# Layer norm's normalisation from VectorE to ScalarE, and tokens and statistics of the QKV stage in another order, in a transformer block on one core

## The chip, the core and the metric

The kernel runs on one core of a Trainium2 chip. The core has a matmul engine (TensorE: PE in the profile, its weight loads PEld), a vector engine (VectorE: DVE), an engine for activations, which computes func(scale * x + bias) with a scale and a bias per partition (ScalarE: ACT), a general engine (GpSimd: POOL), and a queue that only issues transfers (SyncE: SP). Each engine takes its own instructions in order, waits on semaphores for the others, and reads from a working memory of 128 partitions; matmul results go to a small second memory of banks (PSUM). The metric is the device time of one execution in microseconds (us); the time of a kernel is the median of its runs. A profile comes from one execution of its own.

## The reference

The reference is a transformer block whose two layer norms are modulated by a condition. It runs on x of shape (2, 2048, 512) in float32, with 16 heads of 32 channels and a hidden size of 2048:

```python
mod = silu(condition) @ Wada + bada
sh_a, sc_a, gt_a, sh_m, sc_m, gt_m = split(mod, 6, axis=1)
xm = layernorm(x, g1, be1) * (1 + sc_a) + sh_a
x  = x + gt_a * attention(xm, Wqkv, Wproj, bproj)     # causal
xm = layernorm(x, g2, be2) * (1 + sc_m) + sh_m
x  = x + gt_m * (gelu(xm @ W1 + b1) @ W2 + b2)
```

Each layer norm takes the mean and the variance over the 512 channels of a token, subtracts the mean and multiplies by 1 / sqrt(variance + eps). The gains and shifts g, be, sc and sh are folded by the kernel into one scale and one shift per channel (a1, c1, a2, c2), applied after the tokens have been transposed.

## The kernel before

The two batch rows of 2048 tokens go one after the other through three stages, and then the MLP runs over all of them.

**QKV stage** (class `Qkv`). A row has four groups of 512 tokens, a group four tiles of 128. For a group, `norm` makes the normalised, transposed and modulated tokens xmT in two halves: it normalises two tiles in place (x - mean) * rstd (L244), transposes them on PE into PSUM (L211), and returns a function that applies a1 and c1 on the way back, on DVE (L263) and ACT (L268) by turns. `group` then makes 12 products of a group, numbered n = 0 to 11: eight of queries and keys (`ps_qk`, drained by ACT at L833 and by DVE at L834 into a staging tile `hl` of two parts, of which there are four, and stored by SP at L839), then four of values (`ps_v`, drained by ACT at L855 into `vv`). Behind each product, `between(n)` runs. It is there that the next group is made ready: at n = 0 its tokens are requested (`load_x`, L784), at n = 5 and n = 8 its two halves are normalised and transposed. The statistics of a group (`stats`, L215 and L218: bn_stats and bn_aggr on DVE, and then `inv_std`, L221 and L222: the root on ACT, the reciprocal on DVE) are asked for inside `norm` at n = 5 of the group before, for row 0 from its second group on and for row 1 from its third (those of the first group of row 0 are taken at the start, those of the first two of row 1 in the projection stage). After product 1 SP also loads the new group's keys (L316) and queries (L325) back from memory. From a row's second group on, score matmuls (`s<-kst,qst`) are laid between the matmuls of the products from n = 2 on; DVE takes their row maxima (L456 and L461), and PE has two banks for them. In row 1's QKV stage POOL also prepares the MLP's weights, by transfers of its own queue.

**Attention** (`attention_phase`). PE makes scores, exponentials come from ACT (L596), and DVE still takes the maxima of later units. In the last unit `prepare` and `prefetch` load what comes next, among it four tiles in an old query buffer (`next_s`, shown as `qst`): in row 0 the first four token tiles of row 1, in row 1 the first four tiles of the MLP's input (`x1d`).

**Projection** (`project_phase`). Sixteen output tiles, n = 0 to 15; DVE adds the residual (L1052) and takes the statistics of the second norm, and `inv_std` and a further instruction (L1064) leave rstd2 and shift2 = -mean * rstd. Behind tile n, `between(n)` makes the next stage ready: in row 0 the statistics of row 1's first group at n = 0 to 3 and its two halves at n = 5 and 8, and those of the second group's tokens from n = 12 on; in row 1 the first two groups of the MLP (`ln_t`), in halves at n = 5, 7, 11 and 13.

**MLP.** Two passes over 2048 tokens each. The tokens of the second pass are normalised by ACT, two tiles at a time, as scale * x + bias with rstd2 and shift2 (`normed`, L1281).

The order of the instructions on an engine comes from a planner that may move an instruction to where it expects its inputs to be ready. An instruction wrapped in `act(...)` is held in program order among the others of its engine that are so wrapped; matmuls and transposes on PE all are. The normalisation of L244 is not wrapped before the change, so it stands wherever the planner found room on DVE.

Of the kernel before, what the change touches and what calls it, by code (L numbers as in the profile page):

```python
# [17 lines left out]
P = 128  # L18
# [9 lines left out]
def dit_block_kernel(  # L28
# [36 lines left out]
    nc = tc.nc  # L65
    B, T, D = x.shape
# [3 lines left out]
    NT = T // P  # L70
# [3 lines left out]
    MTT = MT // P  # L74
    NG = T // MT
# [5 lines left out]
    const = ctx.enter_context(tc.tile_pool(name="const", bufs=1))  # L81
# [65 lines left out]
    mv1 = const.tile([P, B * NT, 2], F32, tag="mv1", name="mv1")  # L147
    rstd1 = const.tile([P, B * NT], F32, tag="rstd1", name="rstd1")
    mv2 = const.tile([P, B * NT, 2], F32, tag="mv2", name="mv2")
    rstd2 = const.tile([P, B * NT], F32, tag="rstd2", name="rstd2")  # L150
    shift2 = const.tile([P, B * NT], F32, tag="shift2", name="shift2")

    bgate = bp.tile([P, D], F32, tag="bgate", name="bgate")
# [51 lines left out]
    def act(ins):  # L205

        return tc.keep_in_program_order(ins)
# [9 lines left out]
            act(ins)  # L217
        nc.vector.bn_aggr(mv[:, n, :], st)  # L218

    def inv_std(mv, rstd, lo, hi):  # L220
        nc.scalar.activation(rstd[:, lo:hi], mv[:, lo:hi, 1], AF.Sqrt, bias=eps)  # L221
        nc.vector.reciprocal(rstd[:, lo:hi], rstd[:, lo:hi])  # L222

    def rows_of(psum, r, b, tag):

# [1 line left out]
        mm(ps, pick[:, r, b, :], modr, start=True, stop=True)  # L227
        return ps

    def transposed(pool_, psum, xts, n0, mv, rstd, a, c, b, dst, xns=None):  # L230

        count = len(xts)
        per = 512 // (count * P)
        by_act = xns is not None
        xns = xns or []
        for t, xt in enumerate(xts):
            if by_act:  # L240
                continue
            xn = xt
            n = n0 + t
            nc.vector.tensor_scalar(  # L244
                xn, xt, mv[:, n, 0:1], rstd[:, n : n + 1], ALU.subtract, ALU.mult
            )
            xns.append(xn)
        banks = []
        for cc in range(0, C, per):
            ps = psum.tile([P, per, count * P], F32, tag="mm", name="ps_xt")  # L250
            for ci in range(per):
                for t in range(count):
                    transpose(
                        ps[:, ci, t * P : (t + 1) * P],
                        xns[t][:, (cc + ci) * P : (cc + ci + 1) * P],
                    )
            banks.append(ps)

# [13 lines left out]

        return modulate
# [498 lines left out]
    class Qkv:  # L772
# [20 lines left out]
        def stats(self, g, t, keep=False):  # L793

            n0 = self.row.b * NT + g * MTT
            stats(self.qp, self.xts[g][t], n0 + t, mv1, keep)
            if t == MTT - 1:
                inv_std(mv1, rstd1, n0, n0 + MTT)

        def norm(self, g, j):  # L800

            b = self.row.b
            if j == 0:
                if g > b:
                    for t in range(MTT):
                        self.stats(g, t)
                self.xmT[g] = self.qp.tile([P, C, MT], F32, tag="xmT", name="xmT", bufs=2)
            return transposed(
                self.qp, self.psum, self.xts[g][2 * j : 2 * j + 2],
                b * NT + g * MTT + 2 * j, mv1, rstd1, a1, c1, b,  # L810
                self.xmT[g][:, :, j * 2 * P : (j + 1) * 2 * P],
            )

        def group(self, g, hp, between, among):
# [44 lines left out]
        def run(self, hp, also):  # L859

            row = self.row
            for g in range(NG):

                def between(n):
                    if g + 1 < NG:
                        if n == 0 and g + 1 not in self.xts:
                            self.load_x(g + 1)
                        if n in (5, 8):
                            self.norm(g + 1, n // 8)()
                    elif n == 8:  # L870

                        row.rows(0)
                        act(nc.scalar.activation(first, eps, AF.Exp))
                    also(g, n)
# [127 lines left out]
    def project_phase(row, psum, between):  # L1002
# [4 lines left out]
        b = row.b  # L1007
        with pool(f"proj{b}") as pp:
            n = 0
# [50 lines left out]
                    between(n)  # L1060
                    n += 1
        lo, hi = b * NT, (b + 1) * NT
        inv_std(mv2, rstd2, lo, hi)
        nc.vector.scalar_tensor_tensor(  # L1064
            shift2[:, lo:hi], mv2[:, lo:hi, 0], -1.0, rstd2[:, lo:hi], ALU.mult, ALU.mult
        )


    row = Row(0)
# [184 lines left out]
    with ExitStack() as mlp:  # L1254
# [11 lines left out]
        def ln_t(m, g, j, xts, xns=None):  # L1266

            n0 = (2 * m + g) * MTT + 2 * j
            transposed(
                wp, ps_mm, xts, n0, mv2, rstd2, a2, c2, n0 // NT,  # L1270
                xm[:, :, g, j * half_t : (j + 1) * half_t], xns,
            )()

        def normed(m, n, xts):
# [653 lines left out]
```

## Time and profile before

| | |
|---|---|
| median of 3 runs | 2315.9 us (2313.6 to 2324.05) |
| the profiled execution | 2323.64 us, of which 2321.8 us are the span of the profile |
| granted TensorE clock, mean | 0.996 |
| PE busy | 2262.0 us, 97% |
| PEld busy | 1387.3 us, 60% |
| DVE busy | 1579.0 us, 68% |
| POOL busy | 1289.6 us, 56% |
| ACT busy | 915.0 us, 39% |

In the rows of a timeline the first number is the start in us from the beginning of the span, the second the length in us; then come engine, line, operation, output <- input, the shapes, and the count of merged instructions. In square brackets stands how long the engine was idle just before, and after the arrow the instruction that ended this wait. In a table of windows, each row is a stretch of time: its length, the busy us of PE, PEld, DVE, ACT and POOL (with their numbers of instructions), the granted PE clock (1.00 is full speed), the busy share of the transfer engines, and GB/s. A row that counts a group gives the least, median and greatest length in ns and when the first and the last began. Matmuls overlap at their ends, so the lengths of neighbouring rows may add up to more than the time between their starts. Names without a number stand for all buffers of the name.

### The profile page before, as it was taken

What the parts mean: (1) busy time and instruction counts of PE and PEld (TensorE: products, weight loads), DVE (VectorE), ACT (ScalarE), POOL (GpSimd) and SP (SyncE); (2) the same over time, 40 slices, a digit from 0 to 9 for tenths busy, and PEclk for the clock granted to TensorE, in tenths of its full rate; (3) what the DMA queues carried; (4) which work ended last, traced back from release to release, by engine and by line L of the source; (5) the groups of instructions that cost most, each with busy time, mean ns of one, the idle gap of its engine ahead of it and who ended that gap; (6) DMA issues with size and microseconds to landing.
All of it is one profiled execution on the core that took longest, in us unless ns stands there. A gap on an engine that the chain in (4) does not pass through costs nothing. (4 is left out here: it accounts for less than half of the span.)

```text
span 2321.8 us, 33418 instructions
## 1 busy us (share of the span) xinstructions
PE 2262.0 (97%) x12141; PEld 1387.3 (60%) x12141; DVE 1579.0 (68%) x3117; ACT 915.0 (39%) x1744; POOL 1289.6 (56%) x1036
## 2 busy tenths in 40 slices
PE   8999999999999999999999998999999999999998
PEld 3455455455544444454455554446888888788787
DVE  3366776777756635577677777555896876876787
ACT  2112555555555011155555554622332242152230
POOL 1052987878793664468788885554663602602510
PEclk9999999999999999999999999999999999999999
DMA  7577216151224799970522304265376654654543
GB/s 254 185 243 206 56 27 134 29 119 47 84 107 144 234 301 312 330 192 24 119 47 54 89 24 138 78 218 203 119 266 214 207 178 145 202 184 155 199 143 116
DMA packets 118524, 355.60 MB, mean 153 GB/s; under 512 B 14496, under 2 KB 15052, under 8 KB 103640
## 3 DMA queue, kind: packets, MB, share of 16 engines
q1 hardware_dynamic: 107040, 293.64, 42.0%
q0 software_dynamic: 10944, 59.28, 7.0%
q8 instruction: 96, 1.57, 0.3%
q14 instruction: 68, 0.56, 0.1%
q10 hardware_dynamic: 376, 0.55, 0.1%
HBM read 253.80 MB, written 107.48 MB: 156 GB/s over the span
## 5 line engine op out<-in xcount | busy, mean ns | idle before, releaser
L596 ACT ACTIVATE e<-st 128x512 f32<-128x512 f32 (+1 forms) x1152 | 573.7, 579 | 405.5 <-PE st L203 363.6
L461 DVE TENSOR_REDUCE mx<-s 128x1 f32<-128x512 f32 x612 | 413.4, 687 | 190.3 <-PE s L203 189.1
L626 POOL TENSOR_TENSOR ee<-ee,e 128x1024 f32<-128x1024 f32 x212 | 498.8, 2384 | 12.3 <-ACT e L596 12.3
L203 PE MATMUL s<-kst,qst 128*128 128x512 f32 (+3 forms) x1032 | 473.6, 460 | 20.7 <-DVE mx L461 9.9
L203 PE MATMUL st<-qst,kst 128*128 128x512 f32 (+3 forms) x1280 | 401.9, 379 | 0.0
L203 PE MATMUL ps_a<-sum,room 128*128 128x256 f32 x1504 | 357.3, 382 | 8.8 <-DVE c L1412 6.2
L203 PEld LDWEIGHTS ps_a<-sum,room 128*128 128x128 f32 x1504 | 281.3, 190 | 58.5 <-issue 11.4
L203 PE MATMUL o<-e,vv 128*32 128x512 f32 (+3 forms) x2560 | 301.1, 539 | 0.9 <-POOL e L605 0.9
L456 DVE CUSTOM_DVE_ANT_0 junk<-s,causal 128x128 bf16<-128x128 f32 (+3 forms) x420 | 206.2, 491 | 121.8 <-PE s L203 114.1
L203 PEld LDWEIGHTS s<-kst,qst 128*128 128x128 f32 x1032 | 194.6, 189 | 154.8 <-issue 66.1
L203 PEld LDWEIGHTS st<-qst,kst 128*128 128x128 f32 x1280 | 229.5, 189 | 68.9 <-issue 39.6
L626 POOL TENSOR_TENSOR ee<-e 128x1024 f32<-128x1024 f32 x84 | 198.2, 2381 | 123.2 <-ACT e L596 123.2
L203 PE MATMUL ps_qk<-xmT,wqkv 128*128 128x512 f32 x512 | 239.0, 594 | 1.8 <-DVE xmT L263 1.8
L605 POOL TENSOR_SCALAR_AFFINE_SELECT e<-e 128x256 f32<-128x256 f32 x256 | 103.9, 435 | 112.5 <-ACT e L596 110.3
L203 PEld LDWEIGHTS ps_qk<-xmT,wqkv 128*128 128x128 f32 x512 | 93.9, 190 | 97.2 <-issue 90.9
L203 PEld LDWEIGHTS <-sel 32*128 32x128 bf16 x1152 | 29.8, 91 | 197.0 <-issue 194.9
L1640 POOL TENSOR_TENSOR c<-c,h 128x512 f32<-128x512 f32 x40 | 58.0, 1470 | 160.8 <-ACT c L1638 160.8
L203 PE MATMUL ps_b<-sum,room 128*128 128x256 f32 x608 | 143.6, 379 | 0.0
L203 PEld LDWEIGHTS ps_b<-sum,room 128*128 128x128 f32 x608 | 115.0, 190 | 15.4
L203 PE MATMUL ps_v<-wqkv,xmT 128*128 128x512 f32 x256 | 123.7, 600 | 0.0
L203 PE MATMUL st<-fold,sel 32*128 32x512 bf16 (+1 forms) x1152 | 118.5, 373 | 4.3 <-DVE mhl L482 2.8
L203 PEld LDWEIGHTS o<-e,vv 128*32 128x32 f32 x2560 | 61.3, 108 | 98.9 <-issue 80.8
(179 smaller groups left out, 2949.5 us busy)
## 6 DMA issues: line engine op xcount, KB each, us to landing
qst<-q SPq DMA_DIRECT2D x128, 256.0 KB
room<-w1e SPq DMA_DIRECT2D x28, 1024.0 KB
kst<-k SPq DMA_DIRECT2D x24, 1024.0 KB
room<-w1e SPq DMA_DIRECT2D x28, 768.0 KB
room<-w2e SPq DMA_DIRECT2D x21, 1024.0 KB
q<-hl SPq DMA_DIRECT2D x32, 512.0 KB
k<-hl SPq DMA_DIRECT2D x32, 512.0 KB
room<-w2e SPq DMA_DIRECT2D x21, 768.0 KB
```

The source lines that it names most:

```text
L203: return tc.keep_in_program_order(nc.tensor.matmul(*args, **kw))
L456: nc.vector.tensor_tensor_reduce(junk[:, :w], s[:, :w], causal[:, QB - w :], 1.0, MASKED, ALU.add, ALU.max, m,)
L461: nc.vector.tensor_reduce(m, s[:, :w], axis=AX.X, op=ALU.max)
L596: act(nc.scalar.activation(e[:, h % 2, :w], sts[h][:, :w], AF.Exp))
L605: nc.gpsimd.affine_select(d, d, pattern=[[0, 2], [1, P]], compare_op=ALU.is_ge, fill=0.0, base=0, channel_multiplier=-1,)
L626: act(engine.tensor_tensor(dst, x, y, ALU.add))
L1640: nc.gpsimd.tensor_tensor(c, c, piece_of(base, i, t, pair), ALU.add)
```

## The change

Four things are done. `inv_std` can also make shift = -mean * rstd, and does so for the first norm (shift1, a new small tile) as it was done by hand for the second. `transposed` normalises, where it is given a shift, on ACT as rstd * x + shift instead of on DVE, and either form is now held in program order; all calls give the shift but that of row 0's first group, which stays on DVE. The tokens of group g + 2 are requested at n = 9 of group g instead of at n = 0 of group g + 1. The statistics of a row's third and fourth group are taken one tile per product, at n = 1 to 4 of the group before, and held in program order; those of row 0's second group stay together at n = 5, and are held in program order too.

```diff
-    def inv_std(mv, rstd, lo, hi):
+    def inv_std(mv, rstd, lo, hi, shift=None):
         nc.scalar.activation(rstd[:, lo:hi], mv[:, lo:hi, 1], AF.Sqrt, bias=eps)
         nc.vector.reciprocal(rstd[:, lo:hi], rstd[:, lo:hi])
+        if shift is not None:
+            nc.vector.scalar_tensor_tensor(
+                shift[:, lo:hi], mv[:, lo:hi, 0], -1.0, rstd[:, lo:hi], ALU.mult, ALU.mult
+            )
...
         for t, xt in enumerate(xts):
             if by_act:
                 continue
-            xn = xt
             n = n0 + t
-            nc.vector.tensor_scalar(
-                xn, xt, mv[:, n, 0:1], rstd[:, n : n + 1], ALU.subtract, ALU.mult
-            )
-            xns.append(xn)
+            if shift is None:
+                act(
+                    nc.vector.tensor_scalar(
+                        xt, xt, mv[:, n, 0:1], rstd[:, n : n + 1], ALU.subtract, ALU.mult
+                    )
+                )
+            else:
+                act(
+                    nc.scalar.activation(
+                        xt, xt, AF.Identity,
+                        bias=shift[:, n : n + 1], scale=rstd[:, n : n + 1],
+                    )
+                )
+            xns.append(xt)
...
             if t == MTT - 1:
-                inv_std(mv1, rstd1, n0, n0 + MTT)
+                inv_std(mv1, rstd1, n0, n0 + MTT, shift1)
...
             if j == 0:
-                if g > b:
+                if (b, g) == (0, 1):
                     for t in range(MTT):
-                        self.stats(g, t)
+                        self.stats(g, t, True)
...
                 self.xmT[g][:, :, j * 2 * P : (j + 1) * 2 * P],
+                shift=shift1 if b or g else None,
             )
...
                     if g + 1 < NG:
                         if n == 0 and g + 1 not in self.xts:
                             self.load_x(g + 1)
+                        if 1 <= n <= MTT and g >= 1:
+                            self.stats(g + 1, n - 1, True)
                         if n in (5, 8):
                             self.norm(g + 1, n // 8)()
+                        if n == 9 and g + 2 < NG:
+                            self.load_x(g + 2)
...
-        inv_std(mv2, rstd2, lo, hi)
-        nc.vector.scalar_tensor_tensor(
-            shift2[:, lo:hi], mv2[:, lo:hi, 0], -1.0, rstd2[:, lo:hi], ALU.mult, ALU.mult
-        )
+        inv_std(mv2, rstd2, lo, hi, shift2)
...
             transposed(
                 wp, ps_mm, xts, n0, mv2, rstd2, a2, c2, n0 // NT,
-                xm[:, :, g, j * half_t : (j + 1) * half_t], xns,
+                xm[:, :, g, j * half_t : (j + 1) * half_t], xns, shift2,
             )()
```

More of the change, by code (lines that the diff above doesn't have):

```diff
@@ L150, in dit_block_kernel @@
     rstd2 = const.tile([P, B * NT], F32, tag="rstd2", name="rstd2")
+    shift1 = const.tile([P, B * NT], F32, tag="shift1", name="shift1")
     shift2 = const.tile([P, B * NT], F32, tag="shift2", name="shift2")
@@ L228, in rows_of, with transposed @@
         return ps
-    def transposed(pool_, psum, xts, n0, mv, rstd, a, c, b, dst, xns=None):
+    def transposed(pool_, psum, xts, n0, mv, rstd, a, c, b, dst, xns=None, shift=None):
         count = len(xts)
```

## The prediction

> **What bounds the kernel now.** I read, in this order, the shares of the engines, the busy times stage by stage, then PE's idle gaps in order of time, and last what DVE, ACT and the clock do around each gap.
>
> ```profile
> PE 2262.0 (97%) x12141; PEld 1387.3 (60%) x12141; DVE 1579.0 (68%) x3117; ACT 915.0 (39%) x1744; POOL 1289.6 (56%) x1036
> core 0: us, PE busy (x) PEld busy (x) DVE busy (x) ACT busy (x) POOL busy (x), PEclk, DMA share, GB/s
> 19.00:214.00 195.00, 194.94 (x569) 95.23 (x569) 101.22 (x248) 38.59 (x69) 40.67 (x55) 1.00 0.69 216
> 214.00:739.20 525.20, 516.62 (x3666) 260.77 (x3665) 365.08 (x871) 303.68 (x608) 404.28 (x281) 1.00 0.32 81
> 796.90:996.00 199.10, 191.55 (x534) 94.18 (x532) 98.89 (x238) 35.84 (x65) 104.38 (x132) 0.99 0.93 311
> 996.00:1530.70 534.70, 519.52 (x3666) 261.60 (x3665) 371.22 (x875) 304.00 (x608) 404.43 (x281) 0.99 0.32 81
> ```
>
> PE is busy 97% of the span. The stages are the QKV products of batch row 0, its attention, and the same two of row 1. In row 0's QKV stage PE has no gap at all (194.94 of 195.00): whatever makes PE wait there is paid in full. Row 1 runs the same 3666 attention matmuls in 534.70 us that row 0 runs in 525.20, and its QKV stage has 7.55 us of gaps. Here are these gaps, each behind the DVE or ACT row that caused it:
>
> ```profile
> 847.44 0.69 DVE L215 BATCH_NORM_STATS2 stat<-x 128x6 f32<-128x512 f32 x1 [9.05 <-DMA x<-in_x_dram]
> 852.66 0.44 PE L203 MATMUL s<-kst,qst 128*128 128x384 f32 x1 [2.15 <-DVE mx L456]
> 892.21 0.69 DVE L215 BATCH_NORM_STATS2 stat<-x 128x6 f32<-128x512 f32 x1 [5.18 <-DMA x<-in_x_dram]
> 899.39 0.50 PE L203 MATMUL s<-kst,qst 128*128 128x512 f32 x1 [2.61 <-DVE mx L461]
> 933.91 0.60 ACT L833 ACTIVATE hl<-ps_qk 128x512 fp32r<-128x512 f32 x1 [3.98 <-DMA k<-hl]
> 935.88 0.64 PE L203 MATMUL s<-kst,qst 128*128 128x512 f32 x1 [2.79 <-DVE mx L461]
> 1418.62 2.47 DVE L244 TENSOR_SCALAR qst<-qst,mv,rstd 128x512 f32<-128x512 f32 x1 [3.15 <-DMA qst<-x1d]
> 1421.74 0.26 PE L522 MATMUL ps_m<-ident_h,mhl 128*128 128x128 bf16 x1 [4.37 <-DVE mx L461]
> 1431.50 3.79 DVE L244 TENSOR_SCALAR qst<-qst,mv,rstd 128x512 f32<-128x512 f32 x2
> 1435.55 0.50 PE L203 MATMUL s<-kst,qst 128*128 128x512 f32 x1 [2.55 <-DVE mx L456]
> ```
>
> Twice DVE stands at statistics whose tokens have not landed, and the row maxima that free PE's score banks queue behind it. At 933.91 ACT waits for a staging buffer's store. At 1418 and 1431 DVE holds PE up with the MLP's first norm, moved early into the attention.
>
> The clock after a gap, from the same columns (PEclk is the third number from the end):
>
> ```profile
> 846.00:858.00 12.00, 9.85 (x26) 4.42 (x26) 9.35 (x25) 1.98 (x4) 7.60 (x12) 1.00 0.99 338
> 894.00:906.00 12.00, 9.39 (x27) 4.69 (x26) 9.71 (x24) 1.38 (x3) 3.34 (x5) 1.00 0.89 287
> 936.00:939.40 3.40, 3.40 (x7) 1.59 (x7) 2.47 (x9) 0.00 (x0) 3.32 (x3) 0.51 1.01 322
> 1422.00:1428.00 6.00, 6.00 (x23) 2.72 (x23) 5.12 (x10) 2.28 (x4) 2.84 (x2) 0.53 0.44 169
> 1430.00:1440.00 10.00, 7.45 (x47) 3.55 (x50) 9.07 (x15) 4.67 (x10) 5.22 (x3) 1.00 0.22 82
> ```
>
> Gaps of 2.15, 2.61 and 2.55 us leave it at 1.00. Behind 2.79 us it is 0.51 for 3.4 us (1.7 us lost), behind 4.37 us 0.53 for 6 us (2.8 us lost).
>
> **The change, part by part.** *The normalisation on ACT.*
>
> ```profile
> L244 DVE TENSOR_SCALAR x<-x,mv,rstd x28: 531/544/742, 7.7 to 897.6; 128x512 f32<-128x512 f32 x28
> L244 DVE TENSOR_SCALAR qst<-qst,mv,rstd x12: 522/1232/7026, 758.1 to 1570.3; 128x512 f32<-128x512 f32 x12
> ```
>
> Of these 40 DVE instructions, 36 (all but the four of row 0's first group) become ACT activations, kept in program order. The order of ACT's instructions in the changed kernel says where they stand: at product 5 of a group behind that product's own drain (hl), at product 8 behind its drain (vv). PE's order is unchanged: the transposes that read the normalised tiles follow product 5 or 8 directly. So PE ends a product, waits for ACT to drain it and normalise two tiles, and only then goes on.
>
> ```profile
> 817.46 1.04 PE L211 MATMUL ps_xt<-ident,x 128*128 128x128 f32 x8
> 817.66 0.60 ACT L833 ACTIVATE hl<-ps_qk 128x512 fp32r<-128x512 f32 x1 [2.84 <-PE ps_qk L203]
> 828.64 1.04 PE L211 MATMUL ps_xt<-ident,x 128*128 128x128 f32 x8
> 828.84 0.58 ACT L855 COPY vv<-ps_v 128x512 f32<-128x512 f32 x1 [8.55 <-PE ps_v L203]
> 1686.03 1.51 ACT L1281 ACTIVATE xn<-x,shift,rstd 128x512 f32<-128x512 f32 x2
> 102.93 1.09 ACT L833 ACTIVATE hl<-ps_qk 128x512 fp32r<-128x512 f32 x2
> ```
>
> The drain begins 0.20 us after the transposes do now. It takes 0.60, with some 0.10 overlap into the next instruction, and a pair of these very activations takes 1.51 in the MLP. That is 0.20 + 0.50 + 1.51 = 2.21, plus 0.06 until PE wakes, minus the 0.13 by which the second transpose starts later anyway: 2.15 us per site. With the pair as short as two PSUM drains (1.09) it would be 1.73; that is the low end. I take 2.15, the row of the same operation. DVE's shift (0.2 us) ends before ACT's drain in each group and costs nothing.
>
> Each row has six such sites (three groups, two halves). Ten cost 2.15 each, 21.5 us. At product 8 of row 0's second group another hl stands between the vv and the pair: 2.15 + 0.50 = 2.65. The twelfth is row 0's product 5 of the first group.
>
> *The statistics of row 0's second group* are now also in program order, at product 5; before, DVE made them during product 1. All of it falls into the gap:
>
> ```profile
> 39.73 1.04 PE L211 MATMUL ps_xt<-ident,x 128*128 128x128 f32 x8
> 39.98 0.60 ACT L833 ACTIVATE hl<-ps_qk 128x512 fp32r<-128x512 f32 x1 [2.84 <-PE ps_qk L203]
> 36.54 0.60 ACT L833 ACTIVATE hl<-ps_qk 128x512 fp32r<-128x512 f32 x1 [2.88 <-PE ps_qk L203]
> 37.17 0.69 DVE L834 SCALAR_TENSOR_TENSOR hl<-ps_qk,hl 128x512 fp32r<-128x512 f32 x1 [2.79 <-ACT hl L833]
> 895.33 0.18 DVE L218 BATCH_NORM_AGGREGATE mv<-stat 128x2 f32<-128x6 f32 x1
> 799.58 0.30 ACT L221 ACTIVATE rstd<-mv,eps 128x4 f32<-128x4 f32 x1 [0.48 <-DVE mv L218]
> 799.91 0.18 DVE L222 RECIPROCAL rstd<-rstd 128x4 f32<-128x4 f32 x1 [0.22 <-ACT rstd L221]
> 800.13 1.66 DVE L244 TENSOR_SCALAR x<-x,mv,rstd 128x512 f32<-128x512 f32 x3
> ```
>
> ACT drains at 39.98, DVE's half of hl runs from 40.61 to about 41.22, four statistics take 895.51 - 892.21 = 3.30 (to 44.52), the root, the reciprocal and the shift 0.03 + 0.33 + 0.22 + 0.20 (to 45.30), the pair 1.51, the wake 0.06: 46.87 against 39.86, so 7.0 us. The table load ahead of the root runs beside the statistics. After 7.0 us the clock drops; by the 4.37 us row that is 2.8 more (1.7 to 2.8).
>
> [...] The trace has the drop from 2.79 us on. [...]
>
> *Sites without cost.* In row 0's projection stage ACT is idle and normalises between products; in row 1's, four pairs for the MLP stand 7 us or more ahead of their transposes. The first removes a gap:
>
> ```profile
> 759.32 9.81 DVE L244 TENSOR_SCALAR qst<-qst,mv,rstd 128x512 f32<-128x512 f32 x3
> 760.83 0.98 PE L211 MATMUL ps_xt<-ident,qst 128*128 128x128 f32 x7 [0.61 <-DVE qst L244]
> ```
>
> Gain 0.61. If ACT were late there, it would cost a site's 2.15 each. The new shift1 in the start-up delays the first tiles by 0.2 at most.
>
> *The MLP norm out of the attention.* No DVE instruction there waits for x1d any more. Gain: 534.70 - 525.20 = 9.5 us, row 0 being the same stage without it; the parts agree, 4.37 + 2.55 + 2.8 = 9.7. Bounds: nothing, if the maxima are late anyway, to 9.7.
>
> *Tokens requested at product 9, statistics one per product.* On SP's queue the loads move past one q store in row 0; in row 1 they stand where they stood, behind the k store of product 7, but ACT reaches that product's hl about 2 to 4 us earlier in relation to PE. The first statistics wait until product 1 of the next group is drained, two products of 3.44 us (39.98 - 36.54) later than DVE tries them now, so the gaps of 2.15 and 2.61 go: gain 4.76 (bounds 0 to 4.76). Moving a query load ahead of the k store makes that store wait for the q store's landing; nobody needs the keys within the group, cost 0.
>
> *The third gap* hangs on a store that keeps its place. In the changed order ACT has that hl, then the vv, then the pair, so the wait stands straight ahead of the transposes. I count no gain and no loss beyond its 2.15; bounds: 2.79 + 1.7 = 4.5 gained, if the store has landed by then, and 3.98 + 1.7 = 5.7 lost, if ACT waits as long on top.
>
> *Sum*: 21.5 + 2.65 + 7.0 + 2.8 = 33.95 lost, 0.61 + 9.5 + 4.76 = 14.9 gained: +19.1 us. The profiled execution took 2323.64 us, 7.7 above the median of the runs shown (2315.9, from 2313.6 to 2324.05). The same difference on the median gives 2335; if the median run lacks as much of the removed DMA waits as it is shorter, it gives 2342.7. I take 2337.
>
> **The rivals.** *Faster: the pairs do not reach PE.* If ACT ran each pair 2.2 us before PE ends product 5 or 8, the sites would cost nothing and only the gains stand: 2316 - 15 = 2301. The limit is a mean site price of 14.9 / 12 = 1.24 us. For it: ACT is busy 20% of row 0's QKV stage (38.59 of 195). Against: idle or not, ACT takes its instructions in order, and the drain ahead waits for the same product that PE has just ended.
>
> *No change that can be measured.* The third gap goes (4.5), the long gap does not lower the clock (2.8), the pair takes 1.09 (0.42 at 12 sites, 5): 19.1 - 12.3 = +6.8, 2323.
>
> *The clock falls at every site.* Gaps of 2.15 in close succession might count as idleness: 1.7 at each of 11 sites is 19, so 2356. Against: three gaps of 2.15 to 2.61 at full clock. [...]
>
> *The third gap doubles:* 5.7 more, 2343.
>
> **How the numbers follow.** Likeliest 0.58: 2337, by itself 2328 to 2345. Third gap doubled 0.12, clock at every site 0.07, no measurable change 0.15, faster 0.08. About 0.5% (11.6 us, 2304 to 2327) is what a measurement here can tell from no change. Slower is 0.58 + 0.12 + 0.07 = 0.77, same 0.15, faster 0.08. The range 2321 to 2351 holds the likeliest, the doubled gap and most of the no-change case, and leaves out the clock at every site and the faster case.
>
> **What the profile afterwards would show.** PE's transposes of x waiting for ACT x, 12 times, ten near 2.1 us, one near 7 at 40 us with a clock near 0.5 behind it. No wait of DVE statistics for x, no gap of PE near 1420 and 1435 (shifted), row 1's attention within 1 us of row 0's. I would be wrong if the transposes hardly wait for ACT, if row 1's attention keeps its 9.5 us, or if new waits of ACT on stores exceed 6 us.

## The result, and the profile after

| | kernel before | changed kernel |
|---|---|---|
| median of 6 runs | 2316.7 us (2313.6 to 2324.05) | 2340.0 us (2334.3 to 2343.5) |
| ratio to before, 95% interval | | 1.009 (1.0067 to 1.0112) |
| the profiled execution | 2323.64 us | 2342.45 us |

The change makes the kernel slower by 23 us. Of the runs below, one (the pairs behind products 4 and 7) was profiled while the chip ran at a mean clock of 0.56; that execution is used for no number. In the first line of the page of the changed kernel, the work has moved as intended: DVE is busy 31 us less than before, ACT 26 us more. PE has the same 12141 matmuls and is busy 7.6 us longer; 3.3 us of that is the clock (PE worked 19.3 us at half clock in this trace, 12.7 in the first of before), and the section on the long gap and the clock shows where the rest comes from.

```profile
PE 2269.6 (97%) x12141; PEld 1387.5 (59%) x12141; DVE 1547.8 (66%) x3089; ACT 941.2 (40%) x1780; POOL 1290.9 (55%) x1036
```

The same four stages of the changed kernel as the prediction showed of before, as windows:

```profile
18.90:236.50 217.60, 201.61 (x569) 96.95 (x569) 97.19 (x239) 47.40 (x81) 40.54 (x55) 0.98 0.62 194
236.50:762.40 525.90, 517.25 (x3667) 260.65 (x3666) 365.37 (x871) 303.65 (x608) 404.47 (x281) 1.00 0.32 81
819.20:1031.40 212.20, 197.84 (x530) 95.41 (x529) 94.27 (x232) 45.42 (x78) 104.54 (x132) 0.98 0.90 298
1031.40:1555.90 524.50, 516.16 (x3665) 260.56 (x3664) 364.60 (x868) 303.18 (x607) 404.29 (x281) 1.00 0.32 81
```

Row 0's QKV stage is 22.6 us longer than in the first trace of before (217.6 against 195.0), row 1's 13.1 us (212.2 against 199.1); row 1's attention is 10.2 us shorter. The sum of PE's waits for one reason:

```profile
PE ps_xt L212 <- ACT x L256: 25.6, 24, 6.2
```

All 12 sites are there, each as two waits. In order of time, the long gap, the site behind row 0's second group, an ordinary site, and a new gap at the end of row 1's QKV stage:

```profile
41.46 0.60 ACT L848 ACTIVATE hl<-ps_qk 128x512 fp32r<-128x512 f32 x1 [2.84 <-PE ps_qk L204]
46.76 1.52 ACT L256 ACTIVATE x<-x,shift,rstd 128x512 f32<-128x512 f32 x2 [0.45 <-DVE shift L225]
47.62 0.48 PE L212 MATMUL ps_xt<-ident,x 128*128 128x128 f32 x1 [6.20 <-ACT x L256]
115.37 0.33 PE L212 MATMUL ps_xt<-ident,x 128*128 128x128 f32 x1 [1.88 <-ACT x L256]
841.31 0.33 PE L212 MATMUL ps_xt<-ident,x 128*128 128x128 f32 x1 [1.39 <-ACT x L256]
842.01 0.98 PE L212 MATMUL ps_xt<-ident,x 128*128 128x128 f32 x7 [0.38 <-ACT x L256]
1019.39 0.60 ACT L848 ACTIVATE hl<-ps_qk 128x512 fp32r<-128x512 f32 x1 [2.52 <-DMA k<-hl]
1021.37 0.39 PE L204 MATMUL s<-kst,qst 128*128 128x256 f32 x1 [2.15 <-DVE mx L475]
```

At 41.46 ACT drains product 5; the pair starts 5.3 us later, behind the statistics, the root and the shift; PE wakes at 47.62. An ordinary site is a wait of 1.39 us for the first tile (1.15 to 1.44 over these sites) and one of 0.38 for the second. At 1019 ACT waits for a staging buffer's store, which it had done at 933 before; the row maxima and PE wait behind it.

### The profile page after: what moved, and what is told of

The parts are those of the page before. It is cut to its first block, busy times and chain, and to the rows that moved or that the text cites. A ratio compares the mean times of both kernels' runs of the same rounds, so it can differ in the third digit from the quotient of the medians.

```text
span 2340.7 us, 33423 instructions
## 1 busy us (share of the span) xinstructions
PE 2269.6 (97%) x12141; PEld 1387.5 (59%) x12141; DVE 1547.8 (66%) x3089; ACT 941.2 (40%) x1780; POOL 1290.9 (55%) x1036
## 5 line engine op out<-in xcount | busy, mean ns | idle before, releaser
L204 PE MATMUL s<-kst,qst 128*128 128x512 f32 (+3 forms) x1032 | 473.5, 460 | 14.8 <-DVE mx L475 7.9
L204 PE MATMUL ps_qk<-xmT,wqkv 128*128 128x512 f32 x512 | 244.0, 605 | 1.8 <-DVE xmT L277 1.8
L962 POOL DMA_DIRECT2D w<-in_L_cond_W_dram x64 | 41.4, 658 | 143.7 <-DMA kst<-k 127.7
```

Source lines behind the costliest of these rows:

```text
L204: return tc.keep_in_program_order(nc.tensor.matmul(*args, **kw))
L962: nc.gpsimd.dma_start(w[:, n], src)
```

## A second trace of each kernel

The first trace of before was taken 7 us above the median, so both kernels were traced once more. First before, unchanged (one run, 2311.8 us).

> The kernel before once more, for a second trace. Theory (part of what the first trace showed was chance: it was taken at 2323.6 us, 7 us above the median): the two gaps in row 1's attention near 1420 and 1433 us come back, since they hang on DVE's order; the third gap of row 1's QKV stage (2.79 us) and the gaps of 2.36 and 2.33 us in the MLP are gone or smaller, and the profiled time is nearer to 2317. Rival (they are all part of the kernel): all of them come back within 0.5 us.

Row 1's QKV stage, its attention and the MLP in this second trace, as windows:

```profile
798.10:990.30 192.20, 190.06 (x530) 93.40 (x528) 100.41 (x237) 36.30 (x65) 100.65 (x129) 1.00 0.93 314
990.30:1525.20 534.90, 519.67 (x3666) 261.52 (x3665) 371.36 (x875) 304.00 (x608) 408.41 (x285) 0.99 0.33 85
1584.70:2310.00 725.30, 711.65 (x3361) 614.87 (x3359) 556.00 (x727) 218.06 (x372) 262.60 (x213) 1.00 0.54 183
```

Its gaps of PE over 1 us in the first two of these stages, in the timeline:

```profile
897.88 0.50 PE L203 MATMUL s<-kst,qst 128*128 128x512 f32 x1 [1.52 <-DVE mx L461]
1416.11 0.26 PE L522 MATMUL ps_m<-ident_h,mhl 128*128 128x128 bf16 x1 [4.37 <-DVE mx L461]
1430.06 0.51 PE L203 MATMUL s<-kst,qst 128*128 128x512 f32 x1 [2.57 <-DVE mx L456]
```

The attention's two gaps come back to a hundredth of a us, and the stage is 534.9 again. The QKV stage is 192.2 instead of 199.1: of its three gaps (2.15, 2.61 and 2.79 us) one of 1.52 is left. The MLP is 725.3 instead of 731.6. What the first trace had there is, in its window and its timeline:

```profile
1590.20:2321.80 731.60, 713.60 (x3361) 616.04 (x3359) 561.04 (x727) 218.04 (x372) 261.72 (x212) 1.00 0.53 181
```
```profile
2005.35 5.83 DVE L1290 TENSOR_TENSOR sum<-xm 128x256 f32<-128x256 f32 x1
2012.38 0.89 PE L203 MATMUL ps_a<-sum,room 128*128 128x256 f32 x3 [2.36 <-DVE c L1412]
```

And at the same place in the second trace:

```profile
1999.63 0.92 DVE L1290 TENSOR_TENSOR sum<-xm 128x256 f32<-128x256 f32 x1
```

A DVE addition of 256 columns, which took 0.42 us later in the same trace and 0.92 at this place of the second, took 5.83 while POOL added beside it (five additions in 6.20 us from 2002.25 on, and two more in 2.51). The same happened once more at 2187 us (5.81 us), and PE waited 2.36 and 2.33 us, the second time with 1.7 us of low clock behind it. In two of the traces below (row 0's statistics not held; the MLP's norm with the loads) PE's longest wait for DVE c is 2.4 us too, and the MLP takes 728.3 and 730.4 us; in six others, the second trace of before among them, it is 0.9 us and the MLP takes 725.3 to 725.6. So 6.9 us of the QKV stage and 6.3 us of the MLP did not come back, and I take them for chance of that execution.

The changed kernel once more: 2342.4 us (2337.2 to 2346.7), 1.0108 (1.0093 to 1.0123).

> The changed kernel once more, beside the other three on one chip. Theory: about 12 PE waits for ACT x of the same sizes, 23 to 26 us in all; the clock drops behind other sites than in the first trace (855 and 893 us), zero to four of them, on a grid of 3.413 us; the gap of 2.15 us near 1021 us need not come back. Median within 3 us of 2340.

The sites come back (26.8 us in 24 waits), QKV stages of 219.5 and 211.1, attention of row 1 524.6, MLP 725.5. The clock now drops behind the sites near 100 and 116 us and behind one of 2.41 us at 947, instead of those near 855 and 891. The gap near 1021 comes back, as one of 2.18 us at 1023, behind another store. It is not in every execution: in the run with row 0's statistics not held (below), whose row 1 has the same edits, PE has no gap over 0.7 us there.

So the difference has two readings. Against the first trace of before, stage by stage: -0.1 + 22.6 + 0.7 - 0.9 + 13.1 - 10.2 + 0 - 6.3 = 18.9 us, the difference of the spans. Against the second: -0.4 + 20.9 + 0.8 - 0.2 + 20.0 - 10.4 + 0 + 0 = 30.7 us. The medians (23.3 us) lie between.

## Experiments: the parts alone

**The MLP's norm alone** (2305.3 us against 2317.4; 0.9947, 0.9935 to 0.9960). Kernel before with

```diff
+            if shift is None:
+                nc.vector.tensor_scalar(xn, xt, ...)
+            else:
+                act(nc.scalar.activation(xn, xt, AF.Identity, bias=shift[...], scale=rstd[...]))
...
-                xm[:, :, g, j * half_t : (j + 1) * half_t], xns,
+                xm[:, :, g, j * half_t : (j + 1) * half_t], xns, shift2,
```

> The kernel before with one part of the change alone: the MLP's first norm (four pairs, in row 1's projection) on ACT, held in program order; the QKV stages as before. Theory (the DVE norm in row 1's attention held PE up): row 1's attention falls from 534.7 to about 524.5 us, no DVE row there waits for x1d, the four pairs cost nothing in the projection, time 10 us below before, 2306 to 2308. Rival (the row maxima are late there anyway): the stage stays within 2 us of 534.7 and the time within 3 us of before. A second rival, on the MLP, whose length was 726.7 us in the trace before and 720.4 after: if the change shortened it, it is this part that does, and the time is 16 us below before; if it is chance, it comes out anywhere between the two.

Row 1's QKV stage and its attention, as windows:

```profile
797.00:989.80 192.80, 190.14 (x531) 93.46 (x531) 100.48 (x238) 36.21 (x65) 101.97 (x130) 1.00 0.92 309
989.80:1514.80 525.00, 516.73 (x3666) 260.64 (x3665) 365.10 (x871) 303.74 (x608) 407.65 (x284) 1.00 0.33 87
```

The attention falls by 9.7 us, the four pairs cost nothing, and the time falls by 12. This part is right by itself, and it is the fastest kernel of all here. The QKV stage, which this edit does not touch, is 192.8, as in the second trace of before (192.2).

**Loads and statistics alone** (2319.4 us against 2317.4; 1.0010, 1.0001 to 1.0019). Kernel before with

```diff
-                if g > b:
+                if (b, g) == (0, 1):
...
+                        if 1 <= n <= MTT and g >= 1:
+                            self.stats(g + 1, n - 1, True)
...
+                        if n == 9 and g + 2 < NG:
+                            self.load_x(g + 2)
```

> The kernel before with the other part alone: tokens of group g + 2 requested at product 9, and the statistics of a row's third and fourth group one per product, held in program order; every normalisation stays on DVE where the planner puts it. Theory (DVE stood at statistics whose tokens had not landed): no DVE statistic waits for x, PE's gaps of 2.15 and 2.61 us near 852 and 899 are gone, row 1's QKV stage falls from 199.1 to about 194.3, time 4.8 us below before, about 2312. Rival 1 (the wait only moves): gaps of PE behind the row maxima add up to over 6 us in row 1's QKV stage as before, time within 2 us of before. Rival 2 (stores wait for more, because loads go ahead of them): row 0's QKV stage, 195.0 before, gets gaps, and the time is above before by 2 us or more.

Statistics hardly wait for x any more (2.4 us in all), and the time is 2 us longer instead of 4.8 shorter. Instead PE's transposes now wait for the DVE normalisation, which has become late (sum of the waits, and the longest in the timeline):

```profile
PE ps_xt L211 <- DVE x L244: 7.1, 6, 2.4
```
```profile
916.74 1.76 PE L211 MATMUL ps_xt<-ident,x 128*128 128x128 f32 x7 [2.42 <-DVE x L244]
```

Two steps of low clock stand behind that wait. In time and in row 0's stage (2.6 us longer) this is the second rival, but by another mechanism than its stores: in DVE's order the normalisation stands behind the held statistics (their reciprocal ends at 911.8, the first normalisation at 913.9, where it took 1.42 us instead of 0.54), and that is too late for its transposes.

**The MLP's norm, and the loads without the statistics** (2306.5 us; 0.9958, 0.9944 to 0.9972): the fastest kernel with the `load_x` lines of the last diff, no more.

> The kernel before with the MLP's norm on ACT (2305.3, the best so far) and the tokens of group g + 2 requested at product 9, but the statistics left to the planner as before. Theory (in the run of loads and statistics the gain was lost because the held statistics made the DVE normalisation late, 7.1 us of transposes waiting for DVE x): no statistic waits for x, no transposes wait for DVE x, row 1's QKV stage 190 to 193 us; the time 0 to 3 us below 2305. Rival (POOL's preparation of the MLP's weights, which runs beside row 1's QKV stage, ends too late for the attention, as in the run with pairs ahead): a wait of PE for POOL e of 2 to 3 us early in row 1's attention and a time of 2305 to 2309.

No gain, and in row 1 nothing to gain from: the tokens are not requested any earlier there. On SP's queue the four requests stand behind the same k store. From the timeline of the kernel before (first trace), and then of this run:

```profile
838.42 0.36 SPq L839 DMA_DIRECT2D k<-hl  x1
838.87 3.93 SPq L784 DMA_DIRECT2D x<-in_x_dram  x4
```
```profile
840.32 0.36 SPq L847 DMA_DIRECT2D k<-hl  x1
840.78 4.49 SPq L792 DMA_DIRECT2D x<-in_x_dram  x4
```

Row 1's QKV stage begins at 796.9 us in the one and at 798.8 in the other, so both request them 42.0 us into the stage. The statistics, too, stand at the same places of DVE's order. In this execution DVE stood at them for 8.52 us, and the row maxima queued behind it:

```profile
848.81 0.69 DVE L215 BATCH_NORM_STATS2 stat<-x 128x6 f32<-128x512 f32 x1 [8.52 <-DMA x<-in_x_dram]
855.41 0.45 PE L203 MATMUL s<-kst,qst 128*128 128x384 f32 x1 [3.00 <-DVE mx L464]
```

That made the stage 198.1 us, like the first trace of before (a wait of 9.05 us). In the second trace of before and in that of the MLP's norm alone the longest wait of this kind is 4.0 and 4.1 us, with requests at the same point of the stage. The execution profiled here was 6.6 us above the median of its run, so how often the long wait comes is not known.

## Experiments: where the pair stands

**Pairs behind products 4 and 7** (2337.4 us against 2317.4; 1.0086, 1.0072 to 1.0101): with the early statistics of the run that the next section begins with. `normalise` issues the pair on ACT, and `norm` then only transposes:

```diff
-                            self.norm(g + 1, n // 8)()
+                            self.norm(g + 1, n // 8, True)()
+                        if n in (4, 7):
+                            self.normalise(g + 1, n // 7)
```

> The kernel of the run before this one, with each pair of ACT normalisations issued one product ahead of its transposes (behind the drain of product 4 and of product 7 instead of products 5 and 8). Theory (the price of the change is that the pair stands between PE's product and its next transposes, not that ACT is the engine): the transposes do not wait for ACT x, or under 3 us in all, both QKV stages come within 3 us of 195 us, row 1's attention stays near 524.5, and the time is before minus the gains, 2316.7 - 10.2 - 4.8 - 0.7 = about 2301, below both kernels. Rival 1 (the drains and the pair crowd ACT, so that the pair behind product 4, which waits for statistics, root and shift, is still late): six transposes wait 1 to 2 us each, time 2307 to 2313. Rival 2 (what costs is ACT's share as such, or the program order of the statistics on DVE): QKV stages above 205 us each, time above 2320.

The time is above 2320, as the second rival has it, but the run does not test that rival: the pairs hardly moved. In ACT's order of this kernel they stand mostly where they stood, behind the drains of products 5 and 8. The drains are not held in program order, and the pair follows statistics that end only behind product 4; that the planner put the drains first for this reason is my reading of the order, not shown. What is written one product earlier is not done earlier.

**Pairs ahead of the drains** (2308.4 us against 2314.9; 0.9968, 0.9957 to 0.9980): the changed kernel with statistics at products 0 to 3 (row 0's second group: all four at product 1, not held) and pairs asked for at products 3 and 4, through the `normalise` of the run before.

```diff
-                        if 1 <= n <= MTT and g >= 1:
-                            self.stats(g + 1, n - 1, True)
+                        if n < MTT and g >= 1:
+                            self.stats(g + 1, n, True)
+                        if n == 1 and (row.b, g) == (0, 0):
+                            for t in range(MTT):
+                                self.stats(1, t)
...
+                        if n == 3:
+                            self.normalise(g + 1, 0)
+                        if n == 4:
+                            self.normalise(g + 1, 1)
```

> The changed kernel with the statistics of the next group at products 0 to 3 (row 0's second group: all four, not held, at product 1) and the ACT pairs asked for at products 3 and 4, so that in ACT's order the pairs stand ahead of the drains of products 5 and 8 (in the run with pairs behind products 4 and 7 the planner had put them behind those drains again, and the time stayed at 2337). Theory (the price is the place of the pair behind the drain, not the engine): PE's transposes wait under 2 us in all for ACT x, row 0's QKV stage within 3 us of 195.0, row 1's between 193 and 199, row 1's attention near 524.5; time about 2303, 35 us below the changed kernel and below the kernel before. Rival 1 (ACT or the program order of the statistics costs by itself): QKV stages above 205, time above 2325. Rival 2 (the statistics at products 0 to 3 stand at tokens that have not landed, and the row maxima queue behind them): no waits for ACT x, but gaps of PE behind the row maxima of over 4 us in row 1's QKV stage, time 2308 to 2316.

PE no longer waits for ACT x at all, and the QKV stages are 197.7 (1.7 of it from a drop of the clock in the start-up) and 192.4: 20 us each below the changed kernel, with the same instructions on ACT. The price was the place. The time is 5 us above what the theory said, because row 1's attention is 531.1 us instead of 524.5. From the timeline there, and last, for comparison, from that of the MLP's norm alone:

```profile
999.70 0.58 POOL L1036 DMA_DIRECT2D w1e<-w  x1 [0.30 <-POOL w L1003]
1017.03 2.38 POOL L642 TENSOR_TENSOR ee<-e 128x1024 f32<-128x1024 f32 x1 [5.13 <-DMA w1e<-w]
1029.14 2.28 PE L204 MATMUL o<-e,vv 128*32 128x512 f32 x8 [2.56 <-POOL e L621]
```
```profile
992.56 0.58 POOL L1007 DMA_DIRECT2D w1e<-w  x1 [0.30 <-POOL w L974]
```

POOL prepares the MLP's weights beside row 1's QKV stage. Its last weight store goes out 8.5 us after that stage has ended (at 991.2), POOL is still waiting for such a store when the attention needs it, its later work is late, and PE waits 2.56 us, with 1.7 us of clock behind it. That the stage is 20 us shorter is not all of it. With the MLP's norm alone the stage is as short (192.8 us), but its last store goes out 2.8 us after the end (at 989.8), and no wait of PE for POOL is over 0.5 us. Counted from the start of the stage, POOL is done after 201 us here and after 196 there; what takes it 5 us longer is not shown.

**Pairs not held** (2318.6 us; 1.0014, 1.0002 to 1.0026):

```diff
-                act(
-                    nc.scalar.activation(xt, xt, AF.Identity, ...)
-                )
+                nc.scalar.activation(xt, xt, AF.Identity, ...)
```

> The changed kernel with one word taken back: the ACT normalisation is not held in program order (row 0's four statistics at n = 5 still are). The planner then puts 11 of the 12 pairs, or their first tile, ahead of the drain; the one behind row 0's statistics stays. Theory (it is the holding in program order that puts the pair behind the drain): the ordinary sites lose most of their 1.8 us, PE's wait for ACT x falls from 25.6 us to about 8 (the long gap of 6.2 and some second tiles), time about 2312 to 2318. Rival (the pair is slow to reach PE wherever it stands, since ACT has to do it between the drains): the wait for ACT x stays above 18 us and the time above 2330.

```profile
PE ps_xt L212 <- ACT x L255: 8.7, 6, 6.2
```

In the sum of the waits the long gap (6.2) and 2.5 us are left of 25.6. The word `act` alone makes the ordinary sites. The time stays 0.6 us above the range given, since row 1's attention is 534.0: the MLP's first four normalisations, not held either, move back into it (1429 to 1435 us, with a wait of PE of 1.75 us), and POOL is late as above (2.81 us).

**The norm of the QKV stages back on DVE**, not held, the rest as in the changed kernel (2319.2 us; 1.0019, 1.0007 to 1.0031):

```diff
-                shift=shift1 if b or g else None,
```

> The changed kernel with the QKV stages' normalisation back on DVE and not held; the order of loads and statistics and the MLP's norm on ACT stay, and row 0's four statistics stay held at n = 5. Theory: the eleven ordinary sites go, the long gap near 41 to 47 us stays (statistics, root, reciprocal, shift and then two DVE normalisations of 0.53 us instead of 1.5 us of ACT: about 5.5 us, with a drop of the clock), and some transposes wait for DVE x as in the run of the loads and statistics alone (7 us in all there): row 0's QKV stage 203 to 207, row 1's 195 to 200, time 2312 to 2320. Rival (the sites cost little, and what costs is the order of loads and statistics with the long gap): time above 2328.

As expected in the time and in row 0: QKV stages of 206.8 (the long gap is now a wait of 5.8 us for DVE x) and 193.5, row 1's being 1.5 us below the range given. The attention pays for POOL's lateness again (530.2, with a wait of PE of 2.06 us).

## Experiments: the long gap and the clock

**Row 0's statistics at products 1 to 4** (2339.1 us; 1.0092, 1.0078 to 1.0106):

```diff
-                if (b, g) == (0, 1):
-                    for t in range(MTT):
-                        self.stats(g, t, True)
...
-                        if 1 <= n <= MTT and g >= 1:
+                        if 1 <= n <= MTT and g + 1 > row.b:
```

> The changed kernel with the statistics of row 0's second group taken one per product at n = 1 to 4 of the first group, instead of all four at n = 5. Theory (the long gap at 41.3 to 47.6 us is the chain of four statistics, root, reciprocal and shift, and the clock falls behind it): the gap shrinks from 6.2 to about 1.4 us, the clock stays at 1.00 behind it, row 0's QKV stage falls from 217.6 to about 210 us, time 7.5 us below the changed kernel, about 2332.5. Rival (the tokens of that group are what is late): the gap stays above 4 us or moves to an earlier product, time within 3 us of the changed kernel's 2340. Rival on the clock (it falls at ordinary sites too, by chance): this run has drops behind some gaps of 1.2 to 2.1 us, at other places than the changed kernel's 855 and 893 us, each some 1.7 us.

The gap shrinks from 6.20 to 1.44 us as the theory said, yet the time hardly moves. Row 0's QKV stage falls from 217.6 to 213.4 us and not to 210: low clock takes 3.0 us of it in the start-up instead of 1.7, and one step of it still stands behind the gap. Between this execution and the first trace of the changed kernel the 4.2 us are gone again in row 0's projection (0.7 us longer), row 1's QKV stage (0.8) and the MLP (2.9, where PE was idle for 1.94 us between 1670.29 and 1673.71). Row 1's stage is no shorter although no ordinary site lowers the clock in it: a site that took 1.21 us in the first trace took 3.57, with two steps of low clock behind it. The timeline around it:

```profile
936.55 5.06 POOL L982 TENSOR_TENSOR w<-w 128x512 f32<-128x512 f32 x4
937.19 3.10 DVE L225 SCALAR_TENSOR_TENSOR shift<-mv,rstd 128x4 f32<-128x4 f32 x1
940.33 1.52 ACT L256 ACTIVATE x<-x,shift,rstd 128x512 f32<-128x512 f32 x2 [2.25 <-DVE shift L225]
941.20 0.48 PE L212 MATMUL ps_xt<-ident,x 128*128 128x128 f32 x1 [3.57 <-ACT x L256]
```

The new shift, four columns wide and 0.16 us long elsewhere, took 3.10 us beside POOL's additions. In the changed kernel's two traces the same shift took 0.42 and 1.94 us; the 1.94 made the gap of 2.41 us at 947. In all three traces it stands beside four POOL additions of 1.27 us each and ends within 0.1 us of the end of one of them: here at 940.29, with the third addition ending at 940.36 (936.55 + 3 x 1.27); in the second trace of the changed kernel at 946.36, the third at 946.43 (942.62 + 3 x 1.27); in the first at 944.83, the last at 944.81 (939.74 + 5.07). What makes it so long there is not shown. Whether this explains the medians of all five runs of this kernel is not shown.

**Row 0's statistics not held** (2327.6 us against 2342.4 for the changed kernel beside it on the same chip; 1.0052, 1.0038 to 1.0066):

```diff
-                        self.stats(g, t, True)
+                        self.stats(g, t)
```

> The changed kernel with one word taken back: row 0's four statistics at n = 5 are not held in program order. The planner puts them into product 1 again, and then the first pair ahead of the drains of products 3 to 5, so that this site is gone altogether. Asked because the run with those statistics at products 1 to 4 took 4.8 us out of the gap but left the median where it was. Theory (the long gap costs its 6.3 us and mostly two steps of the clock, 3.4 us; the earlier run hid it in chance): 8 to 10 us below the changed kernel of this same call, row 0's QKV stage 207 to 209 us unless the start-up drops the clock again (1.7 to 3.4 more). Rival (something gives the gain back later): within 3 us of the changed kernel.

14.8 us, more than expected; in the trace, the QKV stages as windows:

```profile
18.40:225.10 206.70, 196.94 (x573) 95.15 (x573) 97.51 (x242) 47.83 (x82) 40.72 (x55) 1.00 0.67 205
807.20:1011.10 203.90, 192.38 (x534) 93.45 (x532) 94.17 (x234) 45.20 (x78) 105.91 (x133) 1.00 0.91 303
```

The clock never fell between start and end of this execution, which makes it the measure of an ordinary site: (206.7 - 195.0) over five sites and (203.9 - 192.2) over six are 23.4 / 11 = 2.13 us (2.27 if the gap of 1.52 us in the 192.2 is left out). The waits for ACT x are only 18.7 us, 1.70 a site. The rest is PE being busy longer: 196.94 us against 194.94 in row 0's stage, 0.4 a site, at the same clock.

The long gap is 217.6 - 1.7 (start-up clock) - 206.7 = 9.2 us in the first trace of the changed kernel. The other 5.6 of the 14.8 us are not explained by the edit: row 1's stage, which it does not touch, is 203.9 us here and 211.1 and 212.2 in the two traces of the changed kernel, where the clock fell. Whether that is more than chance is not shown. The run with statistics at products 1 to 4 should have kept most of the 9.2 us. Its row 0 is 6.7 us above this one's: some 2.1 for its sixth site, 3.0 for the start-up clock and 1.7 for the step behind the gap. Its row 1 is 9.1 above, with the long shift and three steps of low clock.

**A longer gap** (2355.3 us; 1.0175, 1.0156 to 1.0194): an ACT pass more per site.

```diff
+                if shift is shift1 and t == 0:
+                    act(nc.scalar.activation(xt, xt, AF.Identity, scale=1.0))
```

> The changed kernel with one more ACT pass, an identity in place on the first tile ahead of each pair, at every site: each gap of PE grows by about 0.75 us, from some 1.77 to 2.5 us in two parts. Theory of the clock, from the traces so far: the granted clock changes only on a grid of 3.413 us, every drop lasts one step of it, and a step in which PE was idle for about 1.8 us or more is followed by one at half clock (1.7 us lost). Then some 8 of the 12 sites are followed by a drop, against 2 or 3 in the changed kernel: 9.0 us of gaps and some 10 us of clock, time about 2358. Rival 1 (only gaps that fill a step, or those over 2.8 us, lower the clock): drops at no more than 3 sites, time about 2349. Rival 2 (the gap is not PE's bound, other work hides it): time within 4 us of 2340.

The clock dropped behind 8 of the 11 ordinary sites. Windows of this trace on the grid:

```profile
157.56:160.97 3.41, 1.19 (x9) 1.00 (x10) 1.56 (x3) 2.46 (x4) 2.94 (x5) 1.00 0.68 254
160.97:164.38 3.41, 3.41 (x8) 1.46 (x6) 1.02 (x4) 1.02 (x2) 3.32 (x5) 0.50 0.71 211
164.38:167.80 3.42, 3.42 (x11) 1.79 (x10) 1.82 (x4) 0.60 (x1) 1.06 (x1) 1.00 0.68 200
```

And of the first trace of the changed kernel, a site without and one with a drop, both of them 1.39 + 0.38 us:

```profile
838.52:841.93 3.41, 1.73 (x5) 0.47 (x3) 0.69 (x1) 1.97 (x3) 0.00 (x0) 1.00 0.95 206
841.93:845.35 3.42, 3.34 (x13) 1.97 (x14) 1.00 (x2) 1.05 (x3) 3.25 (x5) 1.00 1.03 264
...
852.17:855.58 3.41, 1.65 (x6) 0.52 (x5) 0.00 (x0) 2.00 (x3) 1.42 (x3) 1.00 1.03 394
855.58:858.99 3.41, 3.41 (x10) 2.23 (x10) 1.37 (x3) 1.94 (x4) 3.11 (x5) 0.50 0.80 299
858.99:862.41 3.42, 3.42 (x9) 1.52 (x8) 1.00 (x2) 0.76 (x2) 3.26 (x6) 1.00 0.77 255
```

With 1.68 us idle in a step (3.41 - 1.73) the next one was at full clock, with 1.76 (3.41 - 1.65) at half. The time came out 3 us below the expected 2358, above both rivals. So the prediction's rival that the clock falls at every site is nearly what happened with gaps of 2.5 us (8 of 11 sites); with those of 1.77 us, a site with 1.76 us in one step had a drop behind it and one with 1.68 had none.

## Why the prediction was right, and where it was wrong

The time (2337 against 2340.0) and the sign were right, and the main mechanism is shown: holding the pair in program order put it between a product's drain and the transposes, and taking back that hold, or that place, takes the loss away. Point by point:

- **The site's price**, 2.15 us (its terms add up to 2.14): 2.13 measured. The pair took 1.52 us as in the MLP. But the waits for ACT x, foretold "near 2.1 us", are 1.70 us a site; the other 0.4 is PE being busy longer around the wait, which the prediction does not name, so the agreement to 0.02 us is in part luck. The site with another drain ahead (2.65 predicted) waits 1.88 + 0.37 us against 1.39 + 0.38, so 0.48 more, as added.
- **The long gap**, 7.0 + 2.8 us: 9.2 measured. The chain ran as written.
- **The MLP's norm out of the attention**, 9.5 us: 10.2, and 9.7 with this part alone.
- **The projection**, 0.61 us: the first traces of the two kernels differ by 0.9 us in row 0's projection, but the second trace of before has 56.9 us there, against 56.8 and 57.4 of the changed kernel. A gain of this size is not shown.
- **"So the gaps of 2.15 and 2.61 go: gain 4.76"**: this step failed. The gaps shrank to one of 1.52 us in a second trace of the same kernel, and the edit alone gained nothing (2 us lost). One execution's waits for transfers were taken for the kernel's. The fault could be seen beforehand: that execution was 7.7 us above the median.
- **"I count no gain and no loss beyond its 2.15"** for the third gap: the wait for a store left product 5 but came back a group later, 2.15 and 2.18 us near 1021, with 1.7 us of clock once. One of the prediction's signs of being wrong, new waits of ACT on stores of over 6 us, is left undecided: in the first trace of the changed kernel the waits of ACT that end with the landing of a staging store are 8.4 us, against 4.0 in the first trace of before and none in the second.
- **"Gaps of 2.15, 2.61 and 2.55 us leave it at 1.00"**: the rows were read as a threshold in the length of a gap. Two sites with the same gaps of 1.39 + 0.38 us differ in the first trace of the changed kernel: one with 1.76 us idle in a step of 3.41 us had a drop behind it, one with 1.68 none. The changed kernel's two traces lost two steps each to ordinary sites, 3.4 us, where none was counted.
- **"DVE's shift (0.2 us) ... costs nothing"**: true in row 0. In row 1 it took 1.94 us in one trace of the changed kernel, and 3.10 in the run with statistics at products 1 to 4, beside POOL: the work that hides it was named (the drain), but not POOL's additions, beside which it took that long.

That the sum matched the two profiled executions (19.1 against 18.9) was luck: errors met, and against the second trace of before it would have been 12 us too small. There the terms that hold give 21.05 us for row 0's stage (20.9 measured) and 12.9 for row 1's (20.0 measured; two drops and the gaps at the end, 3.4 + 0.7 + 2.15 + 1.7, less the 1.52 that before has there, make 6.4 of the rest), less 10.4 for the attention.

## What to carry to other kernels

An instruction that a busy engine waits for should stand ahead of the work that waits for that same engine's last result; look for its place in the compiled order, since moving the line may do nothing, and holding it in order may do the opposite. Before a wait is counted as a gain, trace the kernel twice: waits for transfers (in row 1's QKV stage they made three gaps of PE of 2.15 to 2.79 us in the first trace of before, one of 1.52 in the second) and DVE instructions beside POOL's additions (5.83 and 0.92 us at the same place) differed between executions here, while those that hang on the order of instructions came back (4.37 us in both). When a stage gets shorter, look at what runs beside it: in three runs here POOL's weights became the next wait (2.06 to 2.81 us).

## What the runs showed of the hardware

The granted clock of PE moved on a grid of 3.413 us. In the first trace of before it falls at 936.09, 1420.78 and 2195.61 us: 484.69 and 774.83 us apart, which is 142 and 227 steps of 3.4133. In every trace with drops, each low stretch between the start-up and the last 20 us is 3.41 us long or a multiple, and all of them in one trace begin at the same phase of these steps. Over thirteen traces (all but that of the pairs behind products 4 and 7), leaving out the first 30 and the last 20 us, 34 steps at full clock were followed by a step at half. All of these had PE idle for 1.75 us or more; all 21 steps with 2.05 us or more were followed by a drop. Of those between 1.75 and 2.01 us, 13 were, and others were not (1.77 and 1.90 us in the first trace of before, 1.79 in that of the changed kernel, 2.01 with the longer gap). What decides among these is open. A step at half clock was followed by full clock when PE was idle under 0.1 us in it (34 of 34), and by half again from 0.45 us on (13 of 13). As an estimate from the step's 3.41 us and the halved clock, a drop costs 1.7 us less half the idle time in it.

So 1.75 us of idleness in a step of 3.41 us was enough once, and a site of 1.77 us halved the clock in one place (1.76 us of it in one step) and not in another (1.68).
